# One graph network kernel: TensorE's order in the edge phase written by hand

## The chip, the core and the metric

The kernel runs on one core of a Trainium2 chip. The metric is device time in microseconds (us): the median of three runs, 7373.27 us (7324.53 to 7373.94). Five engines work beside each other, each in its own order: TensorE (PE, matmuls into the PSUM banks), VectorE (DVE), ScalarE (ACT), GpSimd (POOL, which here issues the indirect DMAs) and SyncE (SP, which issues the plain DMAs).

## The reference

12500 nodes with 64 features, 400000 edges with 32 features, sorted by destination.

```
x_t  = leaky(x @ W1n + b1n) @ W2n + b2n                 # per node
e_t  = leaky(edge_attr @ W1e + b1e) @ W2e + b2e         # per edge
agg  = segment_sum(x_t[src] * e_t * dp_scale, dst)      # edge -> node
x1   = norm(x + norm(x + agg * res_w) * gamma + beta)
deg  = segment_sum(1, dst) + 1 ;  g = x1 / sqrt(deg)
h1   = (A + I) g / deg ;  h2 = (A + I) h1               # A[src, dst] counts edges
out  = norm(x1 + (h2 / sqrt(deg)) @ W.T + b)
```

## The kernel before, in words

**Stages.** A set-up (to about 180 us) makes the node table `xt_tab` and looks up where each block's edges start. The edge phase (to about 6200 us) does three things at once: it turns the edges into messages and sums them by node, it builds the count matrix A in DRAM, and it runs the first hop A g for the columns whose nodes are finished. Then come the end of the first hop, the second hop (about 6400 to 7000 us) and the final norm.

**Edges by quads.** The edges are cut into 261 quads (`NQ`) of 12 chunks of 128, taken from the highest node down (`order`). A quad passes four stages, each a function that is called in one step of the loop `for t in range(NQ + 3)`: `hidden` (L568; two halves, each an fp32 matmul `pw` at L574, ACT's bias at L575, then DVE's leaky step L577), `message` (L584; two halves: a bias matmul L588, six fp32 matmul passes L590, DVE's product with the gathered rows L598), `level1` (L608; 24 matmul passes L623 that sum 128 edges into 32 nodes, and ACT's copy L632) and `level2` (L637; matmuls L652 into the `ring` of node windows). `take` loads a quad ahead of use: 12 gathers on POOL (L553) into one of four `xg` buffers, and the edge features on SP (L565). `PRE = 2` quads are taken ahead.

**Counts by slots.** A node block of four rows is counted in one PSUM bank `pa` of 128 x 391. 6054 slots of up to 128 edges each (`SLOTS`) make one matmul (L839) with two one-hots: `koh` for row and high part of the source (L795, 16 slots at once) and `oh` for the low part (L836, one a slot, in a ring of 11 buffers). A block has 1, 2 or 4 groups of rows (w = 4, 2, 1), each with its own columns of PE's array; the slots of one group come together. `fetch` (POOL) brings the slots' edges, `prepare` makes their keys and transposes them on PE. ACT evicts the bank as fp8 and sums it (L853); eight blocks are stored at once (L862), and DVE looks at their sums in three small steps (L875, L876, L879).

**First hop.** Once a supergroup of up to 14 windows of 128 nodes is counted and its nodes are finished, `hop1` loads the counts back (L1015) and, for each of 25 chunks of 512 columns, adds up its windows in the bank `hacc_p`: one 128-column matmul with the two high parts of g (`hm`, L1033) and a 64-column one with the low part (`lw`, L1045), in the order hm, lw lw, hm for each two windows. ACT evicts (L1084), `combine` turns the two halves over (L1163) and DVE adds (L1168). The second hop does the same product at L1138 and L1149 in batches of 16 windows, with PE's order held to the program's (`manual_schedule`).

**What sets the order.** In the edge phase a planner orders each engine's instructions by a model of the time line. The four stages carry a priority of 500; after each stage the loop calls the generators `adjacency` and `hop1` until a share of the step's budget is used (costs by block, 240 and 700 for the hop, `H_RATE = 4400`). Banks: three for `pa`, one each for `pw`, `pe`, `ring` and `hacc_p`, and one that `pl`, the key transposes and `combine` share.

Of the kernel before, what the change touches and what calls it, by code (L numbers as in the profile page):

```python
# [62 lines left out]
NBIG = 48  # L63
SC = 512
# [62 lines left out]
def _slot_tables():  # L127

    slots = []
    for k in range(NBLK - 1, -1, -1):  # L130
        _, w, caps = BLOCKS[k]
        for g in range(4 // w):
            for j in range(caps[g]):
                slots.append((k, w, g, j, j == caps[g] - 1))
    return slots
# [49 lines left out]
def tile_fast(  # L185
# [74 lines left out]
    xgp = main.enter_context(tc.tile_pool(name="xgp", bufs=4))  # L260
    eap = main.enter_context(tc.tile_pool(name="eap", bufs=3))
# [233 lines left out]
    ohp = counts.enter_context(tc.tile_pool(name="ohp", bufs=11))  # L495
    kohp = counts.enter_context(tc.tile_pool(name="kohp", bufs=3))
    stgp = counts.enter_context(tc.tile_pool(name="stgp", bufs=3))
    psA = main.enter_context(tc.tile_pool(name="psA", bufs=3, space=PSUM))
    psW = main.enter_context(tc.tile_pool(name="psW", bufs=1, space=PSUM))
    psE = main.enter_context(tc.tile_pool(name="psE", bufs=1, space=PSUM))  # L500
    psR = main.enter_context(tc.tile_pool(name="psR", bufs=1, space=PSUM))
    psH = main.enter_context(tc.tile_pool(name="psH", bufs=1, space=PSUM))
    psC = main.enter_context(tc.tile_pool(name="psC", bufs=1, space=PSUM))
# [64 lines left out]
    def hidden(q, h):  # L568
        def f():
            if h == 0:  # L570
                hs[q] = edgep.tile([P, 2, SCC * P], F32, name="z")
            z = hs[q]
            pw = psW.tile([P, SCC * P], F32, name="pw")
            nc.tensor.matmul(pw, w1ab[:, h, :], eas[q], start=True, stop=True)  # L574
            nc.scalar.activation(z[:, h, :], pw, AF.Identity, bias=b1)  # L575
            if h == 1:
                nc.vector.scalar_tensor_tensor(  # L577
                    z, z, SLOPE, z, op0=ALU.mult, op1=ALU.max
                )
                del eas[q]  # L580

        return f

    def message(q, h):  # L584
        def f():
            z = hs[q]
            pe = psE.tile([P, 2, SCC, D], F32, name="pe")
# [20 lines left out]
    def level1(q):  # L608
        def f():
# [9 lines left out]
            pl = psC.tile([P, D + 1], F32, name="pl", tag="pc")  # L619
            m = msgs[q % 3]  # L620
            for s in range(4):
                for c in range(SCC):
                    nc.tensor.matmul(  # L623
                        pl[REL * s : REL * (s + 1), :],
                        oh[:, s * SCC + c, :],
                        m[:, s * SCC + c, :],
                        start=(c == 0),
                        stop=(c == SCC - 1),
                        tile_position=(0, REL * s),
                    )  # L630
# [115 lines left out]
    def prepare(k4):  # L746
# [16 lines left out]
        col = slotp.tile([P, SB4, P], F32, name="scol")  # L763
# [8 lines left out]
        )  # L772
        for i in range(SB4):
            pt = psC.tile([P, 2, P], F32, name="pc")
# [36 lines left out]
    def adjacency():  # L811
        i = 0
        stage = None
        for k in range(NBLK - 1, -1, -1):
            _, w, caps = BLOCKS[k]
            sg = blk_sg(k)
            lo_blk = SGS[sg][0] * 32
            if stage is None:
# [3 lines left out]
                sums = stgp.tile([P, STG], F32, name="sums")  # L822
            pa = psA.tile([P, FB], F32, name="pa")
            for g in range(4 // w):
                rows = slice(g * w * FA, (g + 1) * w * FA)
                for j in range(caps[g]):
# [3 lines left out]
                    if i % (P * SB4) == P * SB4 // 2 and (k4 + 1) * SB4 < NSBP:  # L830
                        prepare(k4 + 1)
                    if i not in koh:
                        key_onehot(i)
# [13 lines left out]
                    i += 1  # L847
            u = k - first
            if k < NBIG:
                nc.vector.tensor_reduce(sums[:, u : u + 1], pa, AX.X, ALU.max)  # L850
                nc.scalar.activation(stage[:, u, :], pa, AF.Identity, saturate=True)
            else:
# [5 lines left out]
                    accum_out=sums[:, u : u + 1],  # L858
                )
            if k == first:  # L860
# [13 lines left out]
                top = stgp.tile([P, 1], F32, name="top")  # L874
                nc.vector.tensor_reduce(top, sums[:, :n], AX.X, ALU.max)  # L875
                nc.vector.tensor_scalar(  # L876
                    top, top, MAXDUP + 0.5, None, op0=ALU.is_gt
                )
                nc.vector.tensor_max(  # L879
                    chk[:, CHK_SG + sg : CHK_SG + sg + 1],  # L880
                    chk[:, CHK_SG + sg : CHK_SG + sg + 1],
                    top,
                )
                stage = None
                if k == lo_blk:
                    a_done[sg] = True
            yield BLOCKS[k][0] + 20
# [5 lines left out]
    def scatter_start(pool, psum, psum1):  # L893
# [12 lines left out]
        for u in range(4):  # L906
            nc.vector.memset(kofs[:, u * SCC : (u + 1) * SCC], float(REL * u))
        spc.update(
            pool=pool, psum=psum, psum1=psum1, tri=tri, spare=spare, kofs=kofs, segs={}
# [51 lines left out]
    def scatter_prep(q, ct, first):  # L961
# [16 lines left out]
        pb = spc["psum1"][0].tile([P, QC], F32, name=spc["psum1"][1])  # L978
# [14 lines left out]
        for u in range(0, QC, 4):  # L993
            pc = spc["psum"][0].tile([P, 4, P], F32, name=spc["psum"][1])
# [15 lines left out]
    def load_adj(pool, sg, c):  # L1010
# [12 lines left out]
        return t  # L1023

    def hop_mms(acc, t, lo, hi, c, first):
# [29 lines left out]
        for i in range(0, n, 2):  # L1055
            mms.append(lambda i=i: hm(i, first and i == 0))
            if i + 1 < n:
                mms.append(lambda i=i: (lw(i), lw(i + 1)))
                mms.append(lambda i=i: hm(i + 1, False))
            else:  # L1060
                mms.append(lambda i=i: lw(i))
        return mms

    def hop1():
        pend = []
        for sg in range(len(SGS)):
# [8 lines left out]
            for c in range(NSC):  # L1075
                if c + 2 < NSC:
                    tiles[c + 2] = load_adj(hopp, sg, c + 2)
                acc = psH.tile([P, SC], F32, name="hacc_p")
                w = min(SC, PITCH - c * SC)
                for f in hop_mms(acc, tiles.pop(c), *SGS[sg], c, True):  # L1080
                    f()
                    yield 240
# [3 lines left out]
                if len(pend) > 1:  # L1086
                    combine(*pend.pop(0))
                    yield 700
        while pend:
            combine(*pend.pop(0))  # L1090
            yield 700
# [13 lines left out]
        for j0 in late + list(range(0, late[0], GB)):  # L1105
            n = min(GB, NW - j0)
            if j0 // GB % 2:
                pc = psH.tile([P, GB, D], F32, name="hacc_p")
            else:
                pc = psC.tile([P, GB, D], F32, name="pc")  # L1110
# [20 lines left out]
            yield 1000  # L1131
# [27 lines left out]
    def combine(ev, c, w):  # L1159
        pc = psC.tile([P, SC // P, D], F32, name="pc")  # L1160
# [21 lines left out]
    a_total = sum(bk[0] + 20 for bk in BLOCKS)  # L1182
# [26 lines left out]
    PRE = 2  # L1209
# [4 lines left out]
    H_RATE = 4400  # L1214
    LEAD = 7
    PRIO = 500
    ZERO = 6
# [3 lines left out]
    sparse = list(range(NQ - 1, Q0 - 1, -1))  # L1221
    for t in range(NQ + 3):
        units = []
        if t + PRE < NQ:
            take(order[t + PRE])
        if t < NQ:
            units += [hidden(order[t], 0), hidden(order[t], 1)]
        if 0 <= t - 1 < NQ:
            units += [message(order[t - 1], 0), message(order[t - 1], 1)]
        if 0 <= t - 2 < NQ:  # L1230
            units += [level1(order[t - 2])]
        if 0 <= t - 3 < NQ:
            units += [level2(order[t - 3])]
# [3 lines left out]
        a_target = a_total * min(1.0, (t + LEAD) / NQ)  # L1237
        a_step = max(0.0, a_target - a_spent) / max(1, len(units))
        h_step = H_RATE / max(1, len(units))
        a_goal, h_budget = a_spent, 0.0  # L1240
        for f in units:
            with tc.high_priority(PRIO):
                f()
            a_goal += a_step
            while a_live and a_spent < a_goal:
                c = next(a_gen, None)
                if c is None:
                    a_live = False
                else:
                    a_spent += c  # L1250
            h_budget += h_step
            while h_live and h_budget > 0:
                try:
# [982 lines left out]
```

## Time and profile before

| | |
|---|---|
| runs | 7373.27, 7324.53, 7373.94 us |
| profiled execution | 7307.16 us, span 7305.0 us |
| granted PE clock over the span | 0.801 |
| POOL gathers L553 | 3125, 1009 ns each |
| DVE one-hots L836 | 6054, 328 ns each |
| ACT evictions L853 | 3077, 504 ns each and 209 for the sum |
| HBM | 95 GB/s over the span |

How to read the lines. A group gives line, engine, operation, what it writes and reads, the shape, the count, then busy time in us and the mean of one in ns, then the engine's idle time just before it with the instruction that ended most of it. A matmul's shape is rows by columns of its weights, then what it writes. A row of stages gives the window, its length, the busy us of PE, PE's weight loads, DVE, ACT and POOL with their counts, the granted clock, the share of DMA and GB/s. A wait is given as who waited, for whom, us in total, times and the longest.

### The profile page before, as it was taken

The numbers are of one execution on the slowest core, as the hardware profiler recorded it, in microseconds if no ns is written. First come the engines' busy times: TensorE is split into PE (matmuls) and PEld (weight loads), VectorE is DVE, ScalarE is ACT, GpSimd is POOL, SyncE is SP. The second block draws the span as 40 slices with busy tenths as digits, with TensorE's granted clock in tenths as the row PEclk, the third lists the DMA queues.
The fourth block names the chain that finished last, engine by engine and source line by source line (L and its number), as shares of the span: only waits on it lengthen the run. The fifth ranks groups of instructions, "written<-read, shape, count | busy, mean of one in ns | idle before, by whom it ended". The sixth has DMA issues, their size and how long they took to land.

```text
span 7305.0 us, 91998 instructions
## 1 busy us (share of the span) xinstructions
PE 5406.8 (74%) x31510; PEld 2960.0 (41%) x31510; DVE 3330.4 (46%) x10617; ACT 2331.9 (32%) x7808; POOL 3925.7 (54%) x3677
## 2 busy tenths in 40 slices
PE   4666877778687776868777777787776776789992
PEld 2333443344343343434333334444344444534441
DVE  4545444545545545454454555555456543510003
ACT  1555444534433333333333343232222111210000
POOL 6555555554554544454444555555555454268885
PEclk6777888788788787778877888888788786599996
DMA  3534444434334333434343433333322222299884
GB/s 93 141 83 96 99 104 92 89 87 97 82 84 88 83 85 76 86 81 92 69 93 79 89 84 82 84 80 76 74 66 51 49 67 72 85 212 203 192 177 104
DMA packets 1258944, 698.98 MB, mean 96 GB/s; under 512 B 607516, under 2 KB 1191424, under 8 KB 1257440
## 3 DMA queue, kind: packets, MB, share of 16 engines
q1 hardware_dynamic: 1097552, 566.52, 31.2%
q0 software_dynamic: 160912, 126.49, 11.9%
q8 instruction: 249, 4.08, 0.2%
q14 instruction: 231, 1.89, 0.1%
HBM read 493.05 MB, written 199.62 MB: 95 GB/s over the span
## 4 chain that ended last, share of the span: by engine, by line
PE 60%; issue 12%; another core or an unknown queue 12%; DVE 5%; ACT 4%; POOL 4%; DMA 2%; SPq 0%; DVEq 0%; POOLq 0%; ACTq 0%
PE pa L839 15%; PE hacc_p L1033 10%; PE hacc_p L1045 6%; PE pw L574 6%; PE pe L590 5%; PE pl L623 5%; POOL hop_tab L1388 4%; PE pc L1163 3%; ACT stage L853 3%; PE acc L1138 3%; PE ring L652 2%; DVE oh L836 2%; PE pe L588 2%; PE acc L1149 1%
## 5 line engine op out<-in xcount | busy, mean ns | idle before, releaser
L553 POOL DMA_INDIRECT xg<-xt_tab,si x3125 | 3154.7, 1009 | 2995.7 <-issue 880.8
L836 DVE TENSOR_SCALAR oh<-iota_b,colT 128x391 bf16<-128x391 bf16 x6054 | 1707.7, 328 | 1710.0 <-PE pa L839 791.5
L853 ACT ACTIVATE stage<-pa 128x391 fp8e4<-128x391 f32 x3077 | 1507.9, 504 | 1930.0 <-PE pa L839 871.8
L839 PE MATMUL pa<-oh,koh 128*64 128x391 bf16 (+2 forms) x6054 | 1484.9, 410 | 726.7 <-issue 417.1
L839 PEld LDWEIGHTS <-koh 128*64 128x64 bf16 (+2 forms) x6054 | 718.7, 178 | 1188.6 <-issue 955.2
L1033 PE MATMUL hacc_p<-at,gp 128*128 128x512 fp8e4 (+1 forms) x2425 | 902.2, 432 | 202.6 <-ACT hev L1084 99.3
L1388 POOL DMA_INDIRECT hop_tab<-tot,first x389 | 605.9, 1558 | 119.4 <-issue 114.3
L574 PE MATMUL pw<-eat,w1ab 128*128 128x384 f32 x1044 | 545.3, 609 | 168.6 <-ACT z L575 85.6
L853 ACT ACTIVATION_READ_ACCUMULATOR stage<-pa 128x1 f32 x3077 | 642.4, 209 | 0.0
L1045 PE MATMUL hacc_p<-at,gp 128*64 128x512 fp8e4 (+1 forms) x2425 | 609.6, 448 | 10.5 <-issue 10.1
L590 PEld LDWEIGHTS pe<-w,z 128*128 128x128 f32 x3132 | 529.0, 230 | 123.7 <-issue 104.5
L590 PE MATMUL pe<-w,z 128*128 128x128 f32 x3132 | 553.5, 316 | 33.3 <-issue 33.1
L575 ACT ACTIVATE z<-pw,b 128x384 f32<-128x384 f32 x522 | 304.6, 584 | 628.8 <-remote 176.3
L623 PE MATMUL pl<-msg,oh 128*32 128x65 f32 x6264 | 419.1, 242 | 77.8 <-issue 65.0
L1045 PEld LDWEIGHTS <-gp 128*64 128x64 bf16 x2425 | 159.5, 113 | 780.3 <-issue 776.2
L652 PE MATMUL ring<-tot,oh 128*128 128x65 f32 x1096 | 205.5, 317 | 306.7 <-ACT tot L632 195.7
L1138 PE MATMUL acc<-at,gp 128*128 128x512 fp8e4 (+1 forms) x1900 | 429.6, 380 | 0.0
L623 PEld LDWEIGHTS pl<-msg,oh 128*32 128x32 f32 x6264 | 301.1, 120 | 236.5 <-issue 166.5
L598 DVE TENSOR_TENSOR msg<-pe,xg 128x384 f32<-128x384 f32 x522 | 287.9, 552 | 232.4 <-remote 107.0
L613 DVE TENSOR_TENSOR oh<-iota_f,rel 128x384 f32<-128x384 f32 x261 | 145.0, 556 | 539.5 <-remote 321.6
L1033 PEld LDWEIGHTS <-gp 128*128 128x128 bf16 x2425 | 179.5, 101 | 420.2 <-issue 399.0
L795 DVE TENSOR_TENSOR koh<-iota_k,keyT 128x1024 bf16<-128x1024 bf16 (+6 forms) x393 | 337.8, 860 | 0.0
(212 smaller groups left out, 4132.7 us busy)
## 6 DMA issues: line engine op xcount, KB each, us to landing
adj<-stage SPq DMA_DIRECT2D x390, 391.0 KB
at<-adj SPq DMA_DIRECT2D x97, 896.0 KB
at<-adj SPq DMA_DIRECT2D x144, 512.0 KB
eat<-in_eaq_dram SPq DMA_DIRECT2D x261, 192.0 KB
xg<-xt_tab,si POOLq DMA_INDIRECT x3125
at<-adj SPq DMA_DIRECT2D x120, 256.0 KB
at<-adj SPq DMA_DIRECT2D x24, 832.0 KB
at<-adj SPq DMA_DIRECT2D x24, 768.0 KB
```

The costliest lines, as they stand in the source:

```text
L553: nc.gpsimd.indirect_dma_start(out=xg[:, i, :], out_offset=None, in_=xt_tab, in_offset=bass.IndirectOffsetOnAxis(ap=si[:, c : c + 1], axis=0),
L574: nc.tensor.matmul(pw, w1ab[:, h, :], eas[q], start=True, stop=True)
L590: nc.tensor.matmul(pe[:, :, c, :], z[:, h, c * P : (c + 1) * P], w2, start=False, stop=(c == SCC - 1),)
L623: nc.tensor.matmul(pl[REL * s : REL * (s + 1), :], oh[:, s * SCC + c, :], m[:, s * SCC + c, :], start=(c == 0), stop=(c == SCC - 1), tile_ ...
L652: nc.tensor.matmul(ring[:, w % RING, :], oh[:, (w - lo) * P : (w - lo + 1) * P], tot, start=False, stop=False, skip_group_check=True,)
L836: nc.vector.tensor_scalar(oh, iota_b, colT[:, i % P : i % P + 1], None, op0=ALU.is_equal)
L839: nc.tensor.matmul(pa[rows, :], koh.pop(i), oh, start=(j == 0), stop=(j == caps[g] - 1), tile_position=(0, rows.start),)
L853: nc.scalar.activation(stage[:, u, :], pa, AF.Identity, saturate=True, accum_out=sums[:, u : u + 1],)
L1033: nc.tensor.matmul(acc[:, :w], gp[:kk, lo + i, 0:2, :].rearrange("p t d -> p (t d)"), t[:kk, i, :w], start=start, stop=False, skip_group_c ...
L1045: nc.tensor.matmul(acc[D * h : D * (h + 1), :w], gp[:kk, lo + i, 2, :], t[:kk, i, :w], start=False, stop=False, skip_group_check=True, til ...
L1138: nc.tensor.matmul(acc[:, :w], gp[:kk, wi, 0:2, :].rearrange("p t d -> p (t d)"), t[:kk, wi - lo, :w], start=first and n == 0, stop=False, ...
L1388: nc.gpsimd.indirect_dma_start(out=hop_tab[(q * QC + i) % HT], out_offset=bass.IndirectOffsetOnAxis(ap=first[:, q - Q0, i : i + 1], axis=0 ...
```

## The change

PE's order in the edge phase becomes that of the program while counts are made; the other engines stay with the planner. Within a step the stages now run as hidden, first message, level 2, second message, level 1, each on the quad whose input a former step made, and each has a weight by which the step's count slots and hop windows are dealt out after it. Hop windows go in batches of eight (`hm` eight times, then `lw` eight times). The slots of a block are dealt over its groups in turn, and a pair of slots is the generator's unit. The hidden layer's two halves use 64 rows of the array each. Level 1 goes over the four segments inside the chunk loop. All PSUM tiles but the ring come from one pool of seven banks. The transposes of `prepare` move to `turn`, 128 slots later. The sums of a supergroup are looked at once. `PRE` goes from 2 to 3, with five `xg` and four `eat` buffers; the one-hot ring from 11 to 13, the key one-hots from 3 to 2; the zero tables start at step 3 instead of 6.

```diff
+PRE = 3
+XGB = PRE + 2
...
-        for g in range(4 // w):
-            for j in range(caps[g]):
-                slots.append((k, w, g, j, j == caps[g] - 1))
+        for j in range(max(caps)):
+            for g in range(4 // w):
+                if j < caps[g]:
+                    slots.append((k, w, g, j, j == caps[g] - 1))
...
-    ohp = counts.enter_context(tc.tile_pool(name="ohp", bufs=11))
-    kohp = counts.enter_context(tc.tile_pool(name="kohp", bufs=3))
+    ohp = counts.enter_context(tc.tile_pool(name="ohp", bufs=13))
+    kohp = counts.enter_context(tc.tile_pool(name="kohp", bufs=2))
...
-    psA = main.enter_context(tc.tile_pool(name="psA", bufs=3, space=PSUM))
-    psW = main.enter_context(tc.tile_pool(name="psW", bufs=1, space=PSUM))
-    psE = main.enter_context(tc.tile_pool(name="psE", bufs=1, space=PSUM))
     psR = main.enter_context(tc.tile_pool(name="psR", bufs=1, space=PSUM))
-    psH = main.enter_context(tc.tile_pool(name="psH", bufs=1, space=PSUM))
-    psC = main.enter_context(tc.tile_pool(name="psC", bufs=1, space=PSUM))
+    banks = main.enter_context(tc.tile_pool(name="banks", bufs=7, space=PSUM))
...
+            pws = [bank([P, SCC * P], f"pw{h}") for h in range(2)]
+            for h in range(2):
+                rows = slice(D * h, D * (h + 1))
+                nc.tensor.matmul(
+                    pws[h],
+                    w1ab[rows, h, :],
+                    ea_q[rows],
+                    start=True,
+                    stop=True,
+                    tile_position=(D * h, 0),
                 )
...
-            for s in range(4):
-                for c in range(SCC):
+            for c in range(SCC):
+                for s in range(4):
...
+                    if i % (P * SB4) == P * SB4 * 3 // 4 and (k4 + 1) * SB4 < NSBP:
+                        turn(k4 + 1)
...
+                    if i % 2 == 0:
+                        yield 2
...
-                top = stgp.tile([P, 1], F32, name="top")
-                nc.vector.tensor_reduce(top, sums[:, :n], AX.X, ALU.max)
-                nc.vector.tensor_scalar(
-                    top, top, MAXDUP + 0.5, None, op0=ALU.is_gt
-                )
-                nc.vector.tensor_max(
...
                 if k == lo_blk:
+                    top = stgp.tile([P, 1], F32, name="top")
+                    nc.vector.tensor_reduce(top, sums, AX.X, ALU.max)
...
-        for i in range(0, n, 2):
-            mms.append(lambda i=i: hm(i, first and i == 0))
-            if i + 1 < n:
-                mms.append(lambda i=i: (lw(i), lw(i + 1)))
-                mms.append(lambda i=i: hm(i + 1, False))
-            else:
-                mms.append(lambda i=i: lw(i))
+        def batch(i0, i1):
+            for i in range(i0, i1):
+                hm(i, first and i == 0)
+            for i in range(i0, i1):
+                lw(i)
+
+        for i in range(0, n, HB):
+            k = min(i + HB, n)
+            mms.append((k - i, lambda i=i, k=k: batch(i, k)))
...
+    tensor.enter_context(tc.manual_schedule(engines={mybir.EngineType.PE}))
     for t in range(NQ + 3):
-        units = []
         if t + PRE < NQ:
             take(order[t + PRE])
+        a_step = max(0.0, a_total * min(1.0, (t + LEAD) / NQ) - a_goal)
+        units = []
         if t < NQ:
-            units += [hidden(order[t], 0), hidden(order[t], 1)]
+            units.append((0.15, hidden(order[t])))
         if 0 <= t - 1 < NQ:
-            units += [message(order[t - 1], 0), message(order[t - 1], 1)]
+            units.append((0.25, message(order[t - 1], 0)))
+        if 0 <= t - 3 < NQ:
+            units.append((0.2, level2(order[t - 3])))
+        if 0 <= t - 1 < NQ:
+            units.append((0.25, message(order[t - 1], 1)))
         if 0 <= t - 2 < NQ:
-            units += [level1(order[t - 2])]
-        if 0 <= t - 3 < NQ:
-            units += [level2(order[t - 3])]
+            units.append((0.15, level1(order[t - 2])))
...
+        share = sum(u[0] for u in units)
+        for n, f in units:
             with tc.high_priority(PRIO):
                 f()
+            advance(a_step * n / share, H_RATE * n / share)
+        if a_live and a_goal >= a_total:
+            advance(4.0, 0.0)
+        if not a_live and tensor is not None:
+            tensor.close()
+            tensor = None
```

`advance(slots, windows)` runs `hop1` until its credit of windows is used (at most 16 are saved up) and then `adjacency` until the slots are made; `H_RATE` is now 13.5 windows a step, and a `combine` counts as 2.6.

## The prediction

> **What bounds the kernel now.** I read the page's engine line first, then the busy time by stage, the chain that ended last, the groups of instructions, TensorE's (PE's) timeline in both hops, and last the waits.
>
> ```profile
> PE 5406.8 (74%) x31510; PEld 2960.0 (41%) x31510; DVE 3330.4 (46%) x10617; ACT 2331.9 (32%) x7808; POOL 3925.7 (54%) x3677
> ```
>
> ```profile
> 182.00:6200.00 6018.00, 4468.51 (x24685) 2453.83 (x24685) 3044.67 (x10021) 2177.56 (x7487) 3082.05 (x3057) 0.80 0.38 84
> 6400.00:7000.00 600.00, 550.73 (x4133) 262.27 (x4135) 30.57 (x64) 46.99 (x97) 473.64 (x315) 0.96 0.89 198
> ```
>
> The columns are PE, PE's weight loads, DVE, ACT, POOL, then granted clock, DMA share and GB/s. The edge phase, 182 to 6200 us, is 82% of the span and the only stage that the change rewrites: 6018 us for 261 quads, 23.1 us a quad. PE is busy 74% of it at a clock of 0.80; in the second hop, whose PE order is already written by hand, 92% at 0.96. The floors of the others lie well under 6018: DVE 3045, ACT 2178, and POOL's 3125 gathers, one every 1.25 us in the timeline, 3906. So PE's own time counts, and what makes it stand.
>
> ```profile
> PE 60%; issue 12%; another core or an unknown queue 12%; DVE 5%; ACT 4%; POOL 4%; DMA 2%; SPq 0%; DVEq 0%; POOLq 0%; ACTq 0%
> ```
>
> ```profile
> L1033 PE MATMUL hacc_p<-at,gp 128*128 128x512 fp8e4 (+1 forms) x2425 | 902.2, 432 | 202.6 <-ACT hev L1084 99.3
> L574 PE MATMUL pw<-eat,w1ab 128*128 128x384 f32 x1044 | 545.3, 609 | 168.6 <-ACT z L575 85.6
> L1045 PE MATMUL hacc_p<-at,gp 128*64 128x512 fp8e4 (+1 forms) x2425 | 609.6, 448 | 10.5 <-issue 10.1
> L623 PE MATMUL pl<-msg,oh 128*32 128x65 f32 x6264 | 419.1, 242 | 77.8 <-issue 65.0
> ```
>
> The same hop product in its two orders, first hop and then second (start, duration, and what ran; the granted clock is 1 in both stretches):
>
> ```profile
> 3018.41 0.60 PE L1033 MATMUL hacc_p<-at,gp 128*128 128x512 fp8e4 x2
> 3018.94 0.41 PE L1045 MATMUL hacc_p<-at,gp 128*64 128x512 fp8e4 x2
> 3019.28 0.60 PE L1033 MATMUL hacc_p<-at,gp 128*128 128x512 fp8e4 x2
> ```
>
> ```profile
> 6499.86 3.62 PE L1138 MATMUL acc<-at,gp 128*128 128x512 fp8e4 x16
> 6503.40 1.92 PE L1149 MATMUL acc<-at,gp 128*64 128x512 fp8e4 x16
> 6505.26 2.98 PE L1138 MATMUL acc<-at,gp 128*128 128x512 fp8e4 x13
> ```
>
> First hop: two windows from 3018.41 to 3019.28, 0.87 us, or 435 ns a window. Second hop: sixteen windows from 6499.86 to 6505.26, 5.40 us, or 338 ns. The difference, 97 ns, is one change of form a window (128 columns to 64 and back for every two).
>
> Where PE stands is stranger:
>
> ```profile
> 3244.00:3258.00 14.00, 10.49 (x72) 6.28 (x72) 12.73 (x49) 8.64 (x32) 10.45 (x10) 1.00 0.50 102
> 3258.00:3279.00 21.00, 0.33 (x1) 0.09 (x1) 1.33 (x3) 0.83 (x3) 13.26 (x14) 0.56 0.13 24
> 3279.00:3293.00 14.00, 13.59 (x55) 7.35 (x55) 6.85 (x25) 4.48 (x17) 0.00 (x0) 0.68 0.12 32
> ```
>
> For 21 us PE, DVE and ACT do nothing and only POOL works, at its gathers; they resume at 3279.1, some 3.6 us after the last gather was issued. The profile calls such waits "remote" or "unknown queue", 11.8% of the chain, 862 us. Over the 190 runs of just twelve gathers I counted, in the instruction records, PE idle 1% of the time in the first 4 us of a run, 61% at 15 to 16 us and 11% at 18 us. So a quad costs PE's work plus a stand at the tail of its gathers. The change keeps 12 gathers a quad at the same pace; I leave this stand as it is, and give its going as a rival.
>
> **The change part by part.** The sum is made against the profiled execution, 7307 us; the median of the three runs, 7373, lies 66 above it.
>
> *Hop batches of eight* in place of alternating windows. 2425 windows x 97 ns = 235 us at full clock; at 0.80, 294. Upper end by the group rows: 902.2/2425 + 609.6/2425 = 623 ns a window now, against the second hop's L1138 and L1149, with forms kept apart 419.9/1824 + 219.9/1824 = 351, or 421 once scaled by 0.96/0.80; 202 x 2425 = 490. I take **-290**, the rows that repeat the same pattern; ends -235 and -490.
>
> *Row halves* for the hidden layer. Each half keeps 384 columns and two passes (fp32 shows two matmuls each), so nothing is saved unless the halves run side by side; no row here has row halves. Bounds: 0, and half of L574, 272. The nearest row is L1045: two 64-column matmuls take 0.41 us where two 128-column ones take 0.60. In strict order only the second pass of one half can meet the first of the other: a quarter, 136, less two changes of form a quad (2 x 97 ns x 261 = 50). I take **-90**.
>
> [...]
>
> *Level 1 in trace order, segments innermost.* The 24 matmuls of a quad go out in 0.96 us where nothing is mixed in (3255.76 in the timeline); L623's busy time a quad is 419.1/261 = 1.61, since the planner mixes count slots in. Ends 0 and -170; **-100**.
>
> *Count slots dealt evenly.* By the slot plan 1501 of 3125 blocks have a single group and 1558 one slot in each group, which alternate already. The other 66 hold 528 of 6054 slots; a 64-column slot costs 215 ns of busy time (728.5/3385), a 128-column one 295 (697.4/2362); 528 x 80 ns: **-40**, ends -40 and 0.
>
> *Other changes of form.* I counted 7285 among 24685 matmuls of the phase, 2957 of them the hop's. By the program's order the rest falls from 4330 to about 14 a step, 3650: 680 x 97 ns at 0.80 = **-80**, ends -80 and 0.
>
> *Seven shared banks.* One bank each for hidden, message, hop and level 1 makes PE wait:
>
> ```profile
> PE pa L839 <- ACT stage L853: 188.1, 131, 9.1
> PE hacc_p L1033 <- ACT hev L1084: 99.3, 28, 10.9
> PE pw L574 <- ACT z L575: 85.6, 36, 8.9
> PE pa L839 <- DVE oh L836: 81.0, 56, 8.1
> PE pe L588 <- DVE msg L598: 16.6, 14, 3.0
> ```
>
> 99.3 + 85.6 + 16.6 = 201 could go. Some of it is the stand under another name, so half, **-100**. The counts lose their private three, so the other end is +188, if their wait on ACT's eviction doubles.
>
> *Sums checked once a supergroup.* Out go 391 each of three DVE steps of about 150 ns, 175 us. DVE is busy half the phase and PE waits for its one-hots only 81 us: **0**, ends 0 and -81. The same cover hides moving the key transposes 128 slots later, and one key buffer fewer. Level 2 a step behind level 1 takes PE off "ring <- ACT tot", 195.7 us; but ACT's copy then waited itself, up to 20.3 us "remote", so the stand only moves to the next instruction: 0.
>
> *Longer gather lead.* Each quad's 12 gathers (POOL) and its edge load (SP) go out a step sooner. DVE's message waits on no gather: its idle time is 232.4 us in all, 107.0 of it "remote", and no DMA of xg stands among what ended the rest. Gain 0. At the start a third quad's 12 gathers pass the slot fetches on POOL, which already follow the first two quads there: 12 x 1.25 = **+15**, end 0. The zero tables on SP start three steps sooner, eight as before: 0.
>
> *PE in trace order.* What stands behind a waiting PE instruction can no longer pass it: everything on PE, and behind it DVE's ring of 13 one-hots and ACT's evictions. For the likeliest case 0; its price is the rival below.
>
> Sum: -290 - 90 - 100 - 40 - 80 - 100 + 15 = -685. 7307 - 685 = 6622 for an execution like the profiled one, 7373 - 685 = **6690** for the median. Ends of the terms alone: from -30 to -1330; not all fall together, so this case's own range is 6350 to 7050.
>
> **The rivals.** *The stand shrinks too* (0.25). For: it sets in while DVE waits for PE; a DVE with 13 buffers and 175 us less to do, and a denser PE, might never get there. Against: gathers and their pace are the same. All 862 us gone: 6690 - 862 = 5830; half: 6260.
>
> *PE waits at each group of slots* (0.20), the one that ends slower. In trace order a step has five groups of count slots; if PE reaches a group before DVE's one-hot or ACT's eviction, it stands for the 1.45 us that such a wait takes now (81.0/56; for ACT 188.1/131 = 1.44). It decides from 685/(261 x 1.45) = 1.8 waits a step. At three: 261 x 3 x 1.45 = 1135, so 7373 - 685 + 1135 = 7820. Against: DVE now waits for PE (791.5 us at L836), not PE for DVE.
>
> *The gain is given back at the gathers* (0.08). If PE, done sooner, only stands longer until the run lands, 7373 less at most 100 us: about 7300. Against: a run and its landing take some 17.5 us by the count above, under the 20.5 that a quad would then have.
>
> The change does what it says for PE alone: DVE and ACT stay with the planner, and the dealt slots were mostly dealt already. That is in the terms.
>
> **How the numbers follow.** The likeliest, 0.47, is 6690. From 5830, the shrinking stand at its full price, to 7450, where the slower rival has two waits a step (7373 - 685 + 757 = 7445), lie all but some 2 in 10. About 1% is what a measurement of this kernel can tell from no change. Faster: 0.47 + 0.25 + half of the last rival, 0.76. Same: its other half, 0.04. Slower: 0.20.
>
> **What would show it.** Right: L1033 and L1045 together near 420 ns a window; L574 near 450 us; L623 near 320; waits of PE on hev and z under 100 us together; the clock still near 0.80 and "unknown queue" still some 11% of the chain. Wrong: "PE pa <- DVE oh" or "<- ACT stage" at several hundred us (the slower rival), stands at the gathers' tail gone and the clock over 0.9 (the first rival), or L1033's mean unchanged, so that the batches are not what costs.

## The result and the profile after

The changed kernel takes 7461.20 us (median of four runs, 7420.14 to 7490.40), the kernel before, run beside it, 7373.60 (7324.53 to 7382.35). The ratio is 1.0128, 95% interval 1.0088 to 1.0167: slower by a little over 1%, against 6690 us predicted, and 11 us above the top of the range. The profiled execution took 7480.72 us, span 7478.6, granted clock 0.751 (0.801 before). Its span is 173.6 us longer than that of the profiled execution before, while the medians differ by 88: the execution profiled before lies 66 us under its median, this one 20 above.

PE's work shrank as forecast. Page of the changed kernel, first the engines, then groups:

```profile
PE 4967.0 (66%) x31510; PEld 2833.6 (38%) x31510; DVE 3216.1 (43%) x9464; ACT 2281.1 (31%) x7808; POOL 3870.2 (52%) x3677
```

```profile
L1067 PE MATMUL hacc_p<-at,gp 128*128 128x512 fp8e4 (+1 forms) x2425 | 771.7, 470 | 106.3 <-issue 33.6
L585 PE MATMUL pw<-eat,w1ab 64*128 64x384 f32 x1044 | 445.9, 696 | 399.1 <-issue 240.1
L638 PE MATMUL pl<-msg,oh 128*32 128x65 f32 x6264 | 217.0, 247 | 366.6 <-issue 161.4
L1079 PE MATMUL hacc_p<-at,gp 128*64 128x512 fp8e4 (+1 forms) x2425 | 373.3, 413 | 18.9 <-issue 18.5
```

A hop window costs (771.7 + 373.3)/2425 = 472 ns of busy time, from 623; the hidden layer 445.9 us, from 545.3; level 1 217.0, from 419.1. But idle time before L585 and L638 rose to 399 and 367 us: PE is done sooner and stands longer. Summed over matmul starts 1 us or less apart, from 200 us to the second hop, PE's flow fell from 4514 to 4076 us, -438 (to 6200 us before and 6350 after it is -462, the figure in the expectations); the longer gaps rose from 1686 to 2307, +621. PE, DVE and ACT idle at once (a stand, counted from half a us on, in the edge phase): some 966 us before, 1460 after. What a stand looks like now, in the timeline of the changed kernel (start, length, what ran; in brackets the idle time before it):

```profile
3013.33 0.94 DVE L595 SCALAR_TENSOR_TENSOR z<-z 128x768 f32<-128x768 f32 x1
...
3014.62 0.88 PE L667 MATMUL ring<-tot,oh 128*128 128x65 f32 x6
3015.39 0.94 POOL L563 DMA_INDIRECT xg<-xt_tab,si  x1 [0.31 <-issue]
...
3015.43 0.44 PE L869 MATMUL pa<-oh,koh 128*64 128x391 bf16 x1
3016.64 0.94 POOL L563 DMA_INDIRECT xg<-xt_tab,si  x1 [0.30 <-issue]
3017.89 0.94 POOL L563 DMA_INDIRECT xg<-xt_tab,si  x1 [0.30 <-issue]
3019.13 0.94 POOL L563 DMA_INDIRECT xg<-xt_tab,si  x1 [0.30 <-issue]
...
3020.35 0.34 ACT L1120 COPY hev<-hacc_p 128x224 f32<-128x224 f32 x1 [7.62 <-remote]
```

This run of gathers began at 3007.34. Eight us into it everything but POOL stands, until ACT and DVE go on at 3020.35, with two gathers of the twelve to go. Over the 176 runs of just twelve gathers (parted where 3.5 us or more lie between two), PE is idle 39% of the time at 5 to 6 us of a run, 51% at 8 to 9, 65% at 14 to 15 and 12% at 18 to 19; the 192 such runs before have 13, 29, 58 and 14%. So the stand now sets in earlier and is mostly over at the same place; about a third of the stands over 3 us, before as after, end while gathers still go out. The waits of the stands grew (changed kernel; 855.3, 470.3 and 321.6 us before):

```profile
POOL xg L563 <- DVE msg L613: 1225.8, 122, 23.9
ACT tot L647 <- remote: 771.5, 92, 30.6
DVE oh L628 <- remote: 710.6, 92, 24.7
```

Seen from POOL, the row of gathers moved only at its start: the 101st begins at 258 us before and at 365 after, and from there to the end of the last one it is 6032 us in both. Executions of one kernel differ by some 60 us (58 in the kernel before, 70 in the changed one), so agreement that close is partly luck.

The difference of the two profiled spans, 173.6 us, splits at two marks that can be found in both traces, the last matmul into the ring and the last step of `gwf`, after which the second hop runs. The edge phase ends at 6427.8 us, not 6361.4: +67. From there to the second hop 166.2 us pass, not 50.4: +116. The rest: -9. That second piece, first before, then after:

```profile
6360.00:6412.00 52.00, 28.36 (x409) 22.25 (x408) 36.27 (x84) 23.91 (x64) 0.00 (x0) 0.73 0.59 155
```

```profile
6428.00:6594.00 166.00, 131.97 (x1064) 93.08 (x1063) 122.37 (x242) 79.62 (x159) 0.00 (x0) 0.57 0.57 165
```

In the 166 us DVE is busy 122 us on 242 instructions: above all it makes the second hop's scatter data (`scatter_store`). That can only begin once all counts are done. The last count's matmul started at 5936 us before, 425 us ahead of the end of the edge phase, so this work lay beside the last quads; now it is at 6305, 123 us ahead.

### The profile page after: what moved, and what is told of

Same layout as the page of the kernel before. It is cut to its first block, busy times and chain, and to the rows that moved or that the text cites. A ratio compares the mean times of both kernels' runs of the same rounds, so it can differ in the third digit from the quotient of the medians.

```text
span 7478.6 us, 92857 instructions
## 1 busy us (share of the span) xinstructions
PE 4967.0 (66%) x31510; PEld 2833.6 (38%) x31510; DVE 3216.1 (43%) x9464; ACT 2281.1 (31%) x7808; POOL 3870.2 (52%) x3677
## 5 line engine op out<-in xcount | busy, mean ns | idle before, releaser
L866 DVE TENSOR_SCALAR oh<-iota_b,colT 128x391 bf16<-128x391 bf16 x6054 | 1669.1, 327 | 1808.7 <-PE pa L869 783.3
L869 PE MATMUL pa<-oh,koh 128*64 128x391 bf16 (+2 forms) x6054 | 1366.9, 401 | 887.2 <-issue 416.6
L1067 PE MATMUL hacc_p<-at,gp 128*128 128x512 fp8e4 (+1 forms) x2425 | 771.7, 470 | 106.3 <-issue 33.6
L585 PE MATMUL pw<-eat,w1ab 64*128 64x384 f32 x1044 | 445.9, 696 | 399.1 <-issue 240.1
L1067 PEld LDWEIGHTS <-gp 128*128 128x128 bf16 x2425 | 281.2, 121 | 474.9 <-issue 343.0
L638 PE MATMUL pl<-msg,oh 128*32 128x65 f32 x6264 | 217.0, 247 | 366.6 <-issue 161.4
L1196 PE MATMUL pc<-twoid,hev 128*128 128x64 f32 x1764 | 312.2, 332 | 118.7 <-issue 85.2
L1079 PE MATMUL hacc_p<-at,gp 128*64 128x512 fp8e4 (+1 forms) x2425 | 373.3, 413 | 18.9 <-issue 18.5
L585 PEld LDWEIGHTS pw<-eat,w1ab 64*128 64x128 f32 x1044 | 155.3, 236 | 580.8 <-issue 338.0
L1120 ACT COPY hev<-hacc_p 128x512 f32<-128x512 f32 (+1 forms) x225 | 129.6, 576 | 770.4 <-remote 301.3
L603 PE MATMUL pe<-b2p,ones_b 128*128 128x384 bf16 x522 | 207.6, 398 | 217.7 <-issue 103.7
```

The source lines that it names most:

```text
L585: nc.tensor.matmul(pws[h], w1ab[rows, h, :], ea_q[rows], start=True, stop=True, tile_position=(D * h, 0),)
L638: nc.tensor.matmul(pl[REL * s : REL * (s + 1), :], oh[:, s * SCC + c, :], m[:, s * SCC + c, :], start=(c == 0), stop=(c == SCC - 1), tile_ ...
L866: nc.vector.tensor_scalar(oh, iota_b, colT[:, i % P : i % P + 1], None, op0=ALU.is_equal)
L869: nc.tensor.matmul(pa[rows, :], koh.pop(i), oh, start=(j == 0), stop=(j == caps[g] - 1), tile_position=(0, rows.start),)
L1067: nc.tensor.matmul(acc[:, :w], gp[:kk, lo + i, 0:2, :].rearrange("p t d -> p (t d)"), t[:kk, i, :w], start=start, stop=False, skip_group_c ...
L1079: nc.tensor.matmul(acc[D * h : D * (h + 1), :w], gp[:kk, lo + i, 2, :], t[:kk, i, :w], start=False, stop=False, skip_group_check=True, til ...
```

## The experiments

Two theories stood at the start. Theory 1: the stands belong to POOL's gathers, and PE's saving was paid back there. Theory 2: PE in program order stands on round trips to ACT and DVE. The experiments ran on five chips; whether the first chip is among them is not on record. On four of them the kernel before took 5301 to 5340 us, on the fifth 7206; each run below is held against the kernel before on its own chip.

### Gathers as plain loads

```diff
-        for i in range(real):
-            nc.gpsimd.indirect_dma_start(out=xg[:, i, :], ...)
+        nc.sync.dma_start(xg[:, :real, :],
+            xt_tab[: P * real].rearrange("(p c) d -> p c d", c=real))
```

> The changed kernel with the 12 gathers of a quad replaced by one plain load of the same bytes on SyncE's queue (the rows are the first 1536 of the node table, not the sources' rows, so the messages are not the reference's). Theory 1: the stands belong to POOL's runs of gathers, and the change's saving on PE (462 us between matmul starts) was paid back there. Then PE, DVE and ACT standing together fall from 1460 us in the edge phase to under 300, the granted clock rises above 0.85, the time falls to 5900 to 6300 us and lies 300 us or more below the kernel before with the same edit. Theory 2: PE in trace order stands on round trips to ACT and DVE, gathers or not. Then over 1000 us of common idle time stay, and the time is 7000 us or more, not below the kernel before with the same edit.

> The kernel before with the same edit (12 gathers replaced by one plain load of the same bytes; messages not the reference's). Theory 1: its 966 us of common idle time fall under 300 and the time to 6300 to 6600 us, some 300 us or more above the changed kernel with this edit. Theory 2: also about 6400 us, since its planner avoids the round trips, but below the changed kernel with this edit.

Measured, beside 5340 us: changed kernel 4326 us, kernel before 5164. Common idle time in the edge phase: 11 and 9 us. The same stages in both, changed kernel first, then the kernel before (line numbers are smaller by four in these files):

```profile
1000.00:3000.00 2000.00, 1982.57 (x17051) 1289.08 (x17048) 1773.95 (x5780) 1217.16 (x4342) 23.86 (x20) 1.00 0.65 160
```

```profile
1000.00:4000.00 3000.00, 2930.26 (x18988) 1640.87 (x18988) 2242.01 (x7759) 1498.18 (x4972) 28.30 (x20) 0.99 0.46 117
```

PE is busy 98 to 99% in both, and the changed one puts 8.5 matmuls through a us against 6.3. Without gathers the change is worth 838 us. Theory 2 falls: in program order PE stands on nothing here. Theory 1 had the direction; its times, 5900 to 6300 and 6300 to 6600 us, were set for the first chip and lie far too high, its 300 us between the two kernels far too low.

### Both kernels unaltered, where there are no stands

> The changed kernel unaltered, run again because in the experiments so far the kernel before took 5340 us and not 7373. Theory 1, now sharper: a quad's twelve gathers on POOL are the floor (3125 x 1.25 us = 3906 us, and POOL was at them for 26 to 36% of the chain in the two altered kernels), so PE's saving cannot show. Where the kernel before takes 5340 us, this one takes 5450 to 5550; where it takes 7373, 7400 to 7500. Theory 2 (trace order alone is dear): 5600 us or more, since both altered kernels, one without trace order, lie at 5484 and 5510.

> The kernel before unaltered, for its profile beside that of the changed kernel. Theory 1: in a time of 5340 us the stand at the tail of the gather runs is gone (common idle time in the edge phase under 300 us, from 966) and POOL goes from one run of gathers to the next; if the time is 7373 us, the stands are as in the first profile.

Measured: 5474 us against 5340, ratio 1.0258 (1.0222 to 1.0295). The kernel before, profiled, has 58 us of common idle time, so the stands of the first chip are not there, and still the change is slower. The changed one has 383 us, now waiting for gathered rows (last two lines). Stages of the kernel before, then of the changed one, a line of each one's chain, and DVE's waits for gathered rows:

```profile
1000.00:4000.00 3000.00, 2882.94 (x18912) 1654.88 (x18910) 2307.59 (x7734) 1498.46 (x5093) 2316.66 (x2243) 0.99 0.53 119
```

```profile
1000.00:4000.00 3000.00, 2487.10 (x18426) 1525.51 (x18425) 2026.16 (x6264) 1343.30 (x4686) 2316.68 (x2242) 0.89 0.51 116
```

```profile
PE 49%; POOL 24%; issue 9%; DVE 8%; DMA 8%; ACT 2%; DVEq 0%; SPq 0%; POOLq 0%; ACTq 0%
```

```profile
POOL 38%; PE 20%; issue 15%; DMA 12%; DVE 8%; ACT 6%; SPq 0%; DVEq 0%; POOLq 0%; ACTq 0%
```

```profile
DVE msg L598 <- DMA xg<-xt_tab,si: 252.4, 108, 7.8
```

```profile
DVE msg L613 <- DMA xg<-xt_tab,si: 669.4, 241, 7.0
```

Look at the last number in brackets: 2243 POOL instructions in 3000 us, and 2242. One follows the other with 0.305 us between: 2316.66 us of work and 2243 such gaps fill the 3000 us. PE's busy time in this stretch is 396 us less, and gathers get through at the same pace, one in 1.36 us (2211 and 2218 of them). POOL is the floor, and the kernel before already lies on it, with PE at 96% beside it: two floors of nearly one height, of which the change lowers one.

What is left is what the change costs, and it is the first chip's sum again. Edge phase 4361.2 to 4408.9 us, +48; from there to the second hop 50.4 to 166.3, +116; the rest -9; together 155. The +48 comes from the start: the first matmul of level 1 runs at 236 us, not 138 (301 and 202 on the first chip), the 101st gather at 288, not 227. 206 count slots now run on PE ahead of the first level 1, where the kernel before ran 15; the first step alone deals out 162, the lead of seven steps. POOL waits for a free `xg` meanwhile and does not get the time back: its 2000th gather is 79 us late.

### Two edits that gain nothing

```diff
-    tensor.enter_context(tc.manual_schedule(engines={mybir.EngineType.PE}))
```

> The changed kernel, but PE's order in the edge phase given back to the planner. If the trace order is what lengthens the stands (as theory 2 says, and one form of theory 1), the common idle time falls from 1460 us to about 1000 and the time to 7000 to 7150 us, the saving on PE being kept. If a denser PE by itself runs the others dry at the gathers (the other form of theory 1), idle time and total stay: 7400 to 7480 us.

```diff
-        xg = xgp.tile([P, QC, D], F32, name="xg")
+        xg = [xgp.tile([P, QC // 2, D], F32, name=f"xg{h}") for h in range(2)]
```

> The changed kernel with a quad's gathered rows in two tiles of six chunks, each freed by its own message half, so that POOL's gathers can go in runs of 6 instead of 12. Theory 1: a stand begins 5 us or more into a run, so shorter runs shorten it: common idle time from 1460 us to about 800, time 6700 to 6900 us. Theory 2: the length of the runs has no say, 7400 to 7500 us.

Measured beside 5340 us: 5510 and 5484 us, against 5474 for the changed kernel unaltered. The numbers expected were for 7373; the reading of both is the same: on POOL's floor neither PE's order nor the grain of the buffers gains anything; the planner's order costs 36 us. `after_planner` shows one thing more: with PE's order back at the planner, 206 slots still run ahead of the first level 1, which still comes at 233 us, and 166 us still pass behind the edge phase. So what the change loses at both ends does not come of the trace order alone.

### Where the counts lie

One line deals out the counts. Four forms of it:

```diff
-        a_step = max(0.0, a_total * min(1.0, (t + LEAD) / NQ) - a_goal)
# after_end
+        ... min(1.0, max((t + LEAD) / NQ, t / (NQ - 24))) - a_goal)
# after_start
+        ... min(1.0, min((t + LEAD) / NQ, (t + 1) / (NQ - 64))) - a_goal)
# after_both
+        ... min(1.0, (t + 1) / (NQ - 24)) - a_goal)
# after_mid, after_mid_halves, after_mid_ticks
+        ... min(1.0, (t + 1) / (NQ - 14)) - a_goal)
```

> The changed kernel, but the counts are dealt out so that they are done 24 quads before the end (kernel before: some 21 quads; changed kernel: 8). Only the late steps carry more. Theory 1 (gathers hold the edge phase, and the preparation of the scatter that used to lie beside the last quads now lies behind them): the end of the edge phase stays, and some 105 us behind it go: 5370 us where the kernel before takes 5340, 7355 where it takes 7373. Rival (the counts' place has no say): 5474 or 7461.

> The changed kernel, but the first steps carry 31 count slots each in place of a lead of seven steps' slots, 162, at once. Theory 1: PE in program order makes the first quads wait behind those slots (first level 1 matmul at 236 us against 138), and the gathers, which wait for buffers, lose 70 us that they never make up. So the edge phase ends 50 to 75 us sooner and the time is 5400 to 5425 us where the kernel before takes 5340, 7385 to 7410 where it takes 7373. Rival (the late start is made up by the faster PE): no change, 5474 or 7461.

> The changed kernel with both edits: counts at an even pace from the first step on, done 24 quads before the end. Theory 1: both gains add, 105 + 60: 5300 to 5320 us where the kernel before takes 5340, so just below both kernels and held there by the gathers' floor; 7280 to 7310 where it takes 7373. Rival: 5474 or 7461.

> The changed kernel with counts at an even pace from the first step, done 14 quads before the end instead of 24 (the former left 165 us between the end of the scatter's preparation and that of the quads, and its denser counts went with slower gathers, 1062 ns against 1021). Theory 1 (gathers are the floor; what lies behind them and what slows them sets the rest): from 5376 us to 5330 to 5350, level with the kernel before at 5340; where the kernel before takes 7373, 7290 to 7330. Rival (the preparation then sticks out behind the quads again): 5380 to 5400, or 7400.

> The changed kernel with the counts' even pace and a quad's gathered rows in two tiles, each freed by its own message half, so that runs of six can take the place of twelve. Where the kernel before takes about 7200 us: 6900 to 7100 if runs of six shorten the stand, 7200 if not. Where it takes 5340: 5330 to 5360, as the even pace alone should give there.

Measured: 5419 (-55), 5432 (-42) and 5376 us (-98, the sum of the two), beside 5336; ratios 1.0154, 1.0172 and 1.0064 (1.0040 to 1.0088), down from 1.0258. So the place of the counts counts at both ends, each time for less than expected. In the profiled execution of `after_start` the first level 1 comes at 184 us, and the edge phase ends 16 us sooner; the 55 and the 42 are between medians of two chips. In `after_end` the piece behind the edge phase shrank from 166 to 51 us, but the edge phase ended 75 us later: with more counts a step a gather took longer (in `after_both`, from 1000 to 3000 us, 1062 ns against 1021 in the changed kernel unaltered). Done 14 quads early instead of 24, with the buffers in halves: `after_mid_halves` 5312 us beside 5301, ratio 1.0024 (1.0011 to 1.0036). `after_mid` came to a chip with stands: 7219 beside 7206, 1.0018 (0.9985 to 1.0052), where the unaltered change had 1.0128 on the first chip. So without stands nearly all of the loss was in the place of the counts; with them it seems so, but the change unaltered did not run on that chip. No version here beats the kernel before.

```diff
+            tick = edgep.tile([1, 1], F32, name="tick")
+            ins = nc.gpsimd.tensor_copy(tick, src).ins      # src: just written by DVE
+            with tc.issue_after(ins):
+                gathers(order[t + PRE], 3 * (i + 1), 3 * (i + 2))
```

> The changed kernel with the counts' even pace (done 14 quads before the end) and a quad's 12 gathers dealt out in threes: after the hidden layer and after each message half POOL copies one element that DVE has just written and only then issues three more gathers, so POOL cannot run 12 in a row ahead of DVE. Theory 1 in the form that the stand grows with the length of a run of gathers: where the kernel before takes about 7200 us, common idle time falls from 1286 us by half or more and the time to 6000 to 6700. If the stand goes by the number of gathers and not by their runs, 7150 to 7300 there. Where the kernel before takes 5340 us, POOL is the floor and the ticks can only cost: 5340 to 5450.

Measured: 5458 us beside 5301, 1.0299, on a chip without stands, where it could tell nothing of them. It shows the price of a tie between POOL and DVE (waits of this kernel):

```profile
ACT z L595 <- POOL tick L1232: 683.4, 191, 10.4
```

The tick reads `z`, so ACT may not write that buffer again until POOL, behind its gathers, has come to it. I had not counted that.

### What each part is worth

These six, each run once, have plain loads, so that PE binds and a part of the change shows at full price; 4326 us is the changed kernel, 5164 the kernel before.

```diff
# after_plain_planner: as above, PE's order to the planner
# before_plain_hop: the batches of hop_mms alone, 360 of cost a window
# after_plain_full
-                nc.tensor.matmul(pws[h], w1ab[rows, h, :], ea_q[rows], ..., tile_position=(D * h, 0))
+                nc.tensor.matmul(pws[h], w1ab[:, h, :], ea_q, start=True, stop=True)
# after_plain_l1
-            for c in range(SCC):
-                for s in range(4):
+            for s in range(4):
+                for c in range(SCC):
# after_plain_banks
+    psA = main.enter_context(tc.tile_pool(name="psA", bufs=3, space=PSUM))   # banks: 4
-            pa = bank([P, FB], "pa")
+            pa = psA.tile([P, FB], F32, name="pa")
# after_plain_slots
-        for j in range(max(caps)):
-            for g in range(4 // w):
+        for g in range(4 // w):
+            for j in range(caps[g]):
```

> The changed kernel with plain loads for gathers (messages not the reference's) and PE's order given back to the planner. Changed kernel with plain loads: 4326 us; kernel before with plain loads: 5164. Theory 1 (PE's saving is in the batches, the row halves and the fewer changes of form): most of the 838 us stays, 4400 to 4700 us. Rival: the trace order itself brings it, 4900 to 5100 us.

> The kernel before with plain loads (messages not the reference's) and the hop's windows in batches of eight, nothing else of the change. The prediction put this part at 290 us with ends of 235 and 490: from 5164 us to 4870, between 4930 and 4670. If the planner mixes other matmuls into the batches, the saving stays below 100: 5060 or more.

> The changed kernel with plain loads (messages not the reference's) and the hidden layer's halves on all 128 rows again, as before. Against 4326 us with row halves: the prediction put this part at 90 us with ends of 0 and 272 (full overlap). So 4416, between 4326 and 4598; near 4600 if the halves run side by side in full.

> The changed kernel with plain loads (messages not the reference's) and level 1 in its old order, chunks innermost. The prediction put level 1 in trace order with segments innermost at 100 us, ends 0 and 170. Against 4326 us: 4426 if the order of the segments earns it; 4326 to 4340 if the saving is the trace order's alone. Where the kernel before takes 7373 us, the same by its own plain-load time, which this run then shows for that case: under 4700 if the stands are the gathers'.

> The changed kernel with plain loads (messages not the reference's) and the seven banks split again: three for the counts alone, four shared by the rest. The prediction put the sharing at 100 us of gain with +188 as the other end. Against 4326 us: 4380 to 4430 if sharing earns it; 4326 or below if the counts did better with three of their own.

> The changed kernel with plain loads (messages not the reference's) and the slots of a block in their old order, group by group. The prediction put the dealing at 40 us, ends 0 and 40: from 4326 us to 4366, no more than 4380. If the row and column groups run side by side far better than the 80 ns a slot that the busy time shows, 4400 or more.

The last three ran where the kernel before takes 7206 us; there the counts begin 41 to 44 us later, behind the 48 gathers of the set-up. So these three are compared by the length from the first count to the last ring matmul, 3161 us in the changed kernel.

| part | forecast | measured |
|---|---|---|
| hop batches (in the kernel before) | 290, ends 235 and 490 | 5164 - 4959 = 205 |
| PE in trace order | 0, or a loss | 4470 - 4326 = 144 gained |
| row halves | 90, ends 0 and 272 | 4413 - 4326 = 87 |
| level 1's segments | 100, ends 0 and 170 | 3228 - 3161 = 67 |
| slots dealt | 40 | 3174 - 3161 = 13 |
| seven shared banks | 100, or 188 lost | 3401 - 3161 = 240, against 3 + 4 |

They add to 756 of the 838, though nothing says that they must. The 13 us of the slots, one run on another chip, cannot be told from none. The 3 + 4 banks are not the kernel before's layout either, so the 240 is the price of this split. Over half of it stands in one wait, shared first, then split:

```profile
PE pa L865 <- ACT stage L882: 35.0, 115, 7.9
```

```profile
PE pa L866 <- ACT stage L883: 170.6, 383, 8.3
```

Three banks of their own were too few for the counts, not too many.

Row halves, with them and without:

```profile
L581 PE MATMUL pw<-eat,w1ab 64*128 64x384 f32 x1044 | 275.9, 543 | 9.1 <-ACT stage L882 8.8
```

```profile
L580 PE MATMUL pw<-eat,w1ab 128*128 128x384 f32 x1044 | 405.9, 511 | 8.2 <-ACT stage L874 7.8
```

1044 passes of 543 ns make 567 us in 275.9 us of busy time, 2.05 to one; with full rows 533 in 405.9, 1.31 to one. So the passes overlap more; 130 us of busy time go, 87 of time.

And the set-up, in two kernels that are the same there, first where the kernel before takes 5340 us, then where it takes 7206:

```profile
20.00:80.00 60.00, 41.03 (x230) 31.43 (x229) 45.89 (x98) 12.34 (x21) 45.42 (x41) 0.81 0.71 192
```

```profile
20.00:80.00 60.00, 16.43 (x63) 10.65 (x61) 9.48 (x25) 3.71 (x7) 39.05 (x42) 0.60 0.23 61
```

POOL issues 41 and 42 instructions in both; beside them the one chip runs 230 matmuls, the other 63. Plain loads took 4383 to 4611 us on the latter chip, with 14 us of common idle time in the edge phase (`after_plain_l1`, `after_plain_slots`), where `after_mid` with its gathers has 1280. So the stands go with the gathers there too. Whether it is the chip itself or something else on it at that time, no run tells.

## Why the prediction was wrong

**What bounds the kernel.** The step that failed is the reading "So PE's own time counts, and what makes it stand", together with "I leave this stand as it is". Every term of the sum is PE time, and every one was taken off the total as if the stand were a constant behind it. Of 685 us forecast, 438 did leave PE's flow on the first chip, and 838 leave the time once gathers are plain loads. With gathers, none of it reaches the end. On the chips without stands POOL's row of gathers is the length of the phase, and PE's 96% in the kernel before was no proof against that: the other engine was at its floor too. On the first chip the stand took the time back, 966 to 1460 us, and the row of gathers kept its 6032 us. The profile had shown POOL busy 3082 of 6018 us, so a saturated POOL could not be read from that chip; that the stand goes mostly by the run of gathers and not by PE's work could, and I had counted it.

**The rivals.** "The gain is given back at the gathers", 0.08 and 7300 us, is what happened, with a loss on top. It was ruled down by "under the 20.5 that a quad would then have": a run with its landing, 17.5 us, fits in a quad, but the quad did not shrink to 20.5; by the row of gathers it took 23.9 us (12 x 6032/3024) in both kernels. "PE waits at each group of slots", the slower rival, did not come: "PE pa <- ACT stage" fell to 128.9 us from 188.1. PE's waits for ACT's `tot` rose to 355 us from 196, at whatever instruction came next; with plain loads 0.4 us is left, so they too were the stand. "The stand shrinks too" went the other way.

**PE in trace order, taken as 0.** As PE time it is a gain of 144 us. The loss lay where I did not look, in where the counts come: the scatter's preparation lost its cover at the end (+116 us on both chips where I have the change unaltered), and the first quads stood behind the first slots (the first level 1 some 98 us later). My sum had only "+15" at the start and nothing for the end. With the planner's order both stay as they are (`after_planner`), so it is not the trace order by itself; why the planner of the kernel before ran the counts elsewhere, by the same lead of seven steps, is not shown.

**The sizes.** Hop batches 205 for 290, under even the nearer end of 235; row halves 87 for 90, level 1 67 for 100, slots 13 for 40: right in kind and mostly high. Banks 240 for 100, by another split than the one replaced. DVE's three steps at 0 and the other changes of form were not priced by themselves; by the traces, changes of form outside the hop fell by some 1100 to 1200, not 680.

**What would show it.** L585 came to 446 us (near 450 was set), L638 to 217 (near 320), the hop to 472 ns a window (near 420). The wait of PE for `hev` at the hop fell to 6.2 us and that for `z` at the hidden layer is gone, but over all lines they are 113 and 58 us, under the counts, the message and level 1 above all: 171, not under 100. "PE pa <- DVE oh" fell to 38.3 us. The clock fell to 0.75 instead of staying at 0.80. The share of "unknown queue" cannot be read: the chain of the changed kernel is lost partway and its shares add to about 39%. One reading was wrong besides: that "no DMA of xg stands among what ended the rest" of DVE's idle time at the message. 21.2 us of it end so, little there, but 252.4 us where there are no stands.

**What stays open.** What holds PE, DVE and ACT during a run of gathers on some chips is not settled, nor why only there, nor what gives the row of gathers its 6032 us on the first chip, where POOL is idle half of the time. The kernels that shorten the runs landed on chips without stands.

## What to carry to other kernels

Before a saving on the busiest engine is taken off the total, replace the next engine's work by something free and time both kernels: here plain loads showed PE's 838 us at once, and that the kernel's time was another thing. Two engines can both be nearly full (PE at 96%, POOL with 0.305 us between its instructions); count instructions in a fixed stretch (2243 and 2242) to see which one sets the pace. When the order of the work is rewritten, ask what ran early or late before, at the start and at the end, and who was covered by it; giving the engine back to the planner did not bring it back here.

## What the hardware showed that I had not expected

One program took 7373 us in the first runs, 7206 on one of the five chips and 5301 to 5340 on the other four; the second hop does not differ so: in the 789 us from its start PE is busy 690.6 us on the first chip and on one of the four, POOL 639. The stretch of gathers by row does: from 1000 to 3000 us the kernel before issues 993 on the first chip and 1482 where it takes 5340 us, at 994 and 1024 ns each.

A gather took longer where DVE's longer steps ran beside it. Where the kernel runs on POOL's floor (the changed kernel at 5474 us) its median is 944 ns, but 398 of 3125 took over 1.2 us: 152 of the 382 that overlap the leaky step L595, 190 of 524 beside the key one-hots L817, and none of the 632 that overlap no work of DVE. The one-hots L866 did little: 4 of the 473 gathers that overlap nothing else of DVE. On the first chip the changed kernel's median is the same; over 1.2 us took 66 of 187 gathers beside L595, 96 of 257 beside L817, none of 1314 with no work of DVE, 14 of 733 beside L866 alone.
